# Two ternary feed-forward stages: input turned by DMA instead of TensorE, and the second product slipped between tiles of the first

## The chip, the cores and the metric

The kernel runs on one core of a Trainium2 chip. A core has five engines with a queue each: TensorE (PE in the profile; its weight loads are PEld), VectorE (DVE), ScalarE (ACT), GpSimd (POOL) and SyncE (SP, whose queue issues DMAs). The metric is the device time of one execution in microseconds (us). Before the change it is 2577.71 us, the median of 3 runs (2575.08 to 2578.1).

## What is computed

The input x has shape (8, 1024, 256), so 8192 tokens of 256 numbers. Six sublayers follow each other, each on a layer norm of x that is added back: a gated feed-forward layer with 4-bit weights, a decaying linear attention, the gated layer again, a ternary feed-forward layer, an attention with compressive memories, and the ternary layer again. The change touches the two ternary layers only:

```python
def _ternary(w):
    scale = jnp.maximum(jnp.mean(jnp.abs(w)), 1e-08)
    return jnp.clip(jnp.round(w / scale), -1.0, 1.0)   # in value
h = jnp.einsum('bsd,fd->bsf', x, _ternary(W1)) + b1    # 256 -> 1024
h = jax.nn.gelu(h, approximate=False)
out = jnp.einsum('bsf,df->bsd', h, _ternary(W2)) + b2  # 1024 -> 256
...
x = x + 0.5 * _L1_ffn_ref(_layernorm(x), W1, b1, W2, b2)
```

The ternary weights are exact in a reduced 32-bit format (fp32r) that TensorE multiplies faster than full fp32. The activations are not, so each is split into a rounded high part and a low part (the rest), and every product runs twice.

## The kernel before

x stays in SBUF for the whole kernel as 16 tiles X[g] of a group of 512 tokens each (128 partitions, G = 4 tiles of 128 tokens, 256 columns). `ffn_ternary(last, after)` (L1176) is called twice: L2093 after the second 4-bit layer, and L2095 as the last stage, where each finished group is also stored (L1273, in the last group tile by tile, L1271).

Its steps for a group g of 16:

- `norm(g)` (L1188): four VectorE instructions L1193 write the normalized tiles into xn, a tile with one buffer that all stages share.
- `norm_turn(g)` (L1205): eight TensorE transposes L1212 bring xn into two PSUM tiles pt. ScalarE rounds each to the high part xh (L1215), and VectorE subtracts it from pt to get the low part xl (L1217).
- `hidden(g)` (L1223): for each of eight slices f of 128 of the 1024 columns, four products L1231 (two halves k of the 256 inputs, xh and xl) into a PSUM tile ph; ScalarE applies Gelu with the bias into an SBUF tile hf (L1239) and rounds it to hh (L1240); VectorE subtracts to get hl (L1242).
- `down(g)` (L1252): for each of the four token tiles, sixteen products L1258 (eight slices, hh and hl) into a PSUM tile po, which VectorE adds to x with the factor 0.5 (L1266).
- `biased(j, g)` (L1200): VectorE adds half the output bias to a tile of x ahead of time (L1203).

The loop L1275 runs over g = 0 to 17; iteration g does norm_turn(g), hidden(g - 1) and down(g - 2). Work for VectorE is put between the slices of hidden as a list `between`: norm(g + 1), a share of the layer-norm statistics (`ln.advance(g)`), and near the end the first statistics of the next stage (`begin`). `PLANS` (L346) says in batches of how many groups the statistics are taken, and by which iteration. A tile's statistics are L235 and L236; a batch ends in twelve small instructions, L248 to L264.

PSUM holds two pt tiles, four ph tiles and two po tiles, eight banks in all.

What sets the order: a framework places the instructions of each engine by its own estimate of when they are ready, in the order written where several are. `order_keeper` (L200) makes a function `pin` that ties an instruction behind the last pinned one on its engine. A stage may enter the list `loose`; pinned instructions then stay behind those pinned before that stage, but are not tied to each other. The ternary stages are loose, and TensorE's instructions in them are not pinned at all, so the framework chooses their order. The engines then run the fixed order, and waits are semaphores.

The 4-bit layers already turn data by DMA (L940, L1116, `dma_start_transpose` on 16-bit data), and the SyncE queue issues those transposes and the stores.

Of the kernel before, what the change touches and what calls it, by code (L numbers as in the profile page):

```python
# [10 lines left out]
F32R = mybir.dt.float32r  # L11
BF16 = mybir.dt.bfloat16
I32 = mybir.dt.int32
AF = mybir.ActivationFunctionType
ALU = mybir.AluOpType
AX = mybir.AxisListType
# [7 lines left out]
G = 4  # L24
# [15 lines left out]
def macaron_kernel(  # L40
# [156 lines left out]
    )  # L197


    def order_keeper():  # L200

        last = {}

        def pin(ins):
            e = ins.ins.engine
            if e in last:
                tc.add_manual_dep(
                    ins.ins, last[e].name,
                    mybir.DependencyInfo(
                        mybir.DependencyClass.NoSync, mybir.DependencyReason.DATA  # L210
                    ),
                    reason="order",
                )
            if not loose:
                last[e] = ins.ins
            return ins

        def behind():

            st = ExitStack()  # L220
            for ins in last.values():
                st.enter_context(tc.issue_after(ins))
            return st

        return pin, behind
# [2 lines left out]

    loose = []
    scratch = []  # L230
    pin, behind = order_keeper()

    def tile_stats(xt, mv):
        st = ln_pool.tile([P, 6], F32, tag="ln_s1", name="ln_s1")
# [33 lines left out]
    def statistics(sizes, dues):  # L268
# [81 lines left out]
        "fp4": ((3, 1, 2, 4, 4, 2), [0 if g < 3 else G * (g - 2) + 2 for g in range(NG)]),  # L350

        "decay": ((2, 2, 4, 4, 4), [max(0, G * g - 5) for g in range(NG)]),
        "ternary": ((2, 2, 4, 4, 4), [max(0, g - 1) for g in range(NG)]),

        "memory": (
            (GB + 3, 3, 4, NG), [max(0, G * (g - GB) - 4) for g in range(NG)]
# [42 lines left out]
    def transpose_group(src, dst, psum, tag, both_act=False, pin=lambda ins: ins):  # L399

        for k in range(2):
            pt = psum.tile([P, TG], F32, tag=tag, name="pt")
            for j in range(G):
                pin(
                    nc.tensor.transpose(
                        pt[:, j * P : (j + 1) * P], src[:, j, k * P : (k + 1) * P], ident
                    )
                )
            if k == 0 or both_act:
                nc.scalar.copy(dst[:, k, :], pt)  # L410
            else:
                pin(nc.vector.tensor_copy(dst[:, k, :], pt))

    def fp4_first(xn, mg, pool):

# [760 lines left out]
    def ffn_ternary(last, after=None):  # L1176
        with ExitStack() as st:
            lnp = st.enter_context(tc.tile_pool(name="f1_ln", bufs=2))
            hp = st.enter_context(tc.tile_pool(name="f1_h", bufs=2))
            tp = st.enter_context(tc.tile_pool(name="f1_t", bufs=4))  # L1180
            ps_t = st.enter_context(tc.tile_pool(name="f1_pt", bufs=2, space=PSUM))
            ps_h = st.enter_context(tc.tile_pool(name="f1_ph", bufs=4, space=PSUM))
            ps_o = st.enter_context(tc.tile_pool(name="f1_po", bufs=2, space=PSUM))
            xns, xts, hs = {}, {}, {}
            ln, xns[0] = begun.pop("ternary")
            loose.append("ternary")

            def norm(g):  # L1188
                xn = xn_pool.tile([P, G, D], F32, tag="xn", name="xn")
                for j in range(G):  # L1190
                    n = G * g + j
                    pin(
                        nc.vector.tensor_scalar(  # L1193
                            xn[:, j, :], X[g][:, j, :], ln.mv[:, n, 0:1], ln.lr[:, n : n + 1],
                            ALU.subtract, ALU.mult,
                        )
                    )
                xns[g] = xn

            def biased(j, g):  # L1200

# [3 lines left out]
            def norm_turn(g):  # L1205
                xn = xns.pop(g)
                xh = lnp.tile([P, 2, TG], F32R, tag="xh", name="xh")
                xl = lnp.tile([P, 2, TG], F32R, tag="xl", name="xl")
                for k in range(2):
                    pt = ps_t.tile([P, TG], F32, tag="pt", name="pt")  # L1210
                    for j in range(G):
                        nc.tensor.transpose(  # L1212
                            pt[:, j * P : (j + 1) * P], xn[:, j, k * P : (k + 1) * P], ident
                        )
                    nc.scalar.copy(xh[:, k, :], pt)  # L1215
                    pin(
# [1 line left out]
                            xl[:, k, :], pt, xh[:, k, :].bitcast(F32), ALU.subtract  # L1218
                        )
                    )  # L1220
                xts[g] = (xh, xl)

            def hidden(g, between):  # L1223
                xh, xl = xts.pop(g)
                hh = hp.tile([P, NF, TG], F32R, tag="hh", name="hh")
                hl = hp.tile([P, NF, TG], F32R, tag="hl", name="hl")
                for f in range(NF):
                    ph = ps_h.tile([P, TG], F32, tag="ph", name="ph")
                    for k in range(2):
                        for xt in (xh, xl):  # L1230
                            nc.tensor.matmul(  # L1231
                                ph,
                                lhsT=w1[:, k, f * P : (f + 1) * P],
                                rhs=xt[:, k, :],
                                start=(k == 0 and xt is xh),
                                stop=(k == 1 and xt is xl),
                            )
                    hf = tp.tile([P, TG], F32, tag="hf", name="hf")
                    nc.scalar.activation(hf, ph, AF.Gelu, bias=b1c[:, f : f + 1])  # L1239
                    nc.scalar.copy(hh[:, f, :], hf)  # L1240
                    pin(
                        nc.vector.tensor_tensor(  # L1242
                            hl[:, f, :], hf, hh[:, f, :].bitcast(F32), ALU.subtract
                        )
                    )
                    if f < len(between):
                        between[f]()
                    elif f >= NF - G:
                        biased(f - NF + G, g)
                hs[g] = (hh, hl)  # L1250

            def down(g):  # L1252
                hh, hl = hs.pop(g)
                for j in range(G):
                    po = ps_o.tile([P, D], F32, tag="po", name="po")
                    for f in range(NF):
                        for ht in (hh, hl):
                            nc.tensor.matmul(  # L1258
                                po,
                                lhsT=ht[:, f, j * P : (j + 1) * P],  # L1260
                                rhs=w2[:, f, :],
                                start=(f == 0 and ht is hh),
                                stop=(f == NF - 1 and ht is hl),
                            )
                    pin(
                        nc.vector.scalar_tensor_tensor(  # L1266
# [2 lines left out]
                    )  # L1269
                    if last and g == NG - 1:  # L1270
                        nc.sync.dma_start(out=out_v[g][:, j, :], in_=X[g][:, j, :])  # L1271
                if last and g < NG - 1:
                    nc.sync.dma_start(out=out_v[g], in_=X[g])  # L1273

            for g in range(NG + 2):  # L1275
                between = []
                if g < NG:
                    norm_turn(g)
                    if g + 1 < NG:
                        between.append(lambda: norm(g + 1))  # L1280
                    between.append(lambda: ln.advance(g))
                    if after and g >= NG - 6:
                        between.append(lambda: begin(after, NG - g))
                if 0 <= g - 1 < NG:
                    hidden(g - 1, between)
                else:
                    for do in between:
                        do()
                if 0 <= g - 2 < NG:
                    down(g - 2)  # L1290
            loose.pop()


# [850 lines left out]
```

## Time and profile before

| | |
|---|---|
| median of 3 runs | 2577.71 us (2575.08 to 2578.1) |
| the profiled execution | 2575.58 us |
| its span, first to last instruction | 2573.8 us, mean granted TensorE clock 0.994 |
| first ternary stage, first to last product (L1231 to L1258) | 1473.06 to 1729.76 us |
| second ternary stage | 2312.70 to 2570.11 us |

The profile is of one execution. Busy time is counted per engine; idle time in front of a group of instructions is put down to what ended it. The chain of work that ended last is followed back from the last instruction, at each step to what released it. Matmul records overlap, because TensorE is pipelined: the distance between starts is what a product costs. VectorE instructions that follow each other without a wait overlap a little too.

### The profile page before, as it was taken

To read this page: it belongs to the slowest core of one execution; us is meant where nothing else is said; L and a number is where in the kernel's file an instruction comes from. 1 tells how busy PE (TensorE), PEld (TensorE's weight loads), DVE (VectorE), ACT (ScalarE), POOL (GpSimd) and SP (SyncE) were. 2 spreads that over 40 slices of the span, in tenths; PEclk is the share of its full clock that TensorE was granted. 3 is DMA by queue.
4 is the path that set the end of the run, shared out by engine and by line. 5 is a ranking of instruction groups with operands and counts; after the bars stand their busy time and mean duration, and the time that the engine had idled before them with its cause. 6 is when DMAs were issued, how large, how long until landed. Compare 5 with 4: busy or idle time off the path is not lost.

```text
span 2573.8 us, 53038 instructions
## 1 busy us (share of the span) xinstructions
PE 2477.9 (96%) x20426; PEld 1848.8 (72%) x20426; DVE 2082.0 (81%) x4809; ACT 1245.3 (48%) x2906; POOL 1019.4 (40%) x1282
## 2 busy tenths in 40 slices
PE   4899999989999999999999999999999999999999
PEld 2577777756666666677777689985666767778998
DVE  7798888758878778998888599648888888879864
ACT  5344444433333333444444376656555555437664
POOL 5677676621101004666667400005555555530000
PEclk9999999999999999999999999999999999999999
DMA  7456556500000002565566200000000000000101
GB/s 223 86 120 118 111 122 118 107 21 15 12 21 14 2 2 49 116 121 116 118 118 119 52 1 1 1 1 2 2 2 2 2 2 2 2 2 26 34 33 42
DMA packets 199901, 132.43 MB, mean 51 GB/s; under 512 B 138048, under 2 KB 174944, under 8 KB 199648
## 3 DMA queue, kind: packets, MB, share of 16 engines
q1 hardware_dynamic: 198704, 127.85, 23.2%
q8 instruction: 160, 2.62, 0.4%
q14 instruction: 93, 0.76, 0.1%
q0 software_dynamic: 240, 0.54, 0.1%
q10 hardware_dynamic: 704, 0.66, 0.1%
HBM read 80.77 MB, written 16.52 MB: 38 GB/s over the span
## 4 chain that ended last, share of the span: by engine, by line
PE 79%; DVE 12%; issue 3%; POOL 3%; ACT 3%; DMA 1%; SPq 0%; ACTq 0%; DVEq 0%; POOLq 0%
PE po L1258 9%; PE po L1001 9%; PE ph L1231 9%; PE pu L889 8%; PE pg L889 8%; PE sc L1301 5%; PE py L1385 5%; PE pq L1399 4%; PE pkv L1399 4%; PE pk L1399 4%; PE po L1399 4%; PE py L1367 2%; PE pmo L1824 2%; DVE at L1310 1%; DVE qp L823 1%
## 5 line engine op out<-in xcount | busy, mean ns | idle before, releaser
L889 PE MATMUL pu<-wgu,xt 128*128 128x352 f32 x1024 | 346.9, 461 | 9.2 <-DVE h L904 8.9
L889 PE MATMUL pg<-wgu,xt 128*128 128x352 f32 x1024 | 347.6, 462 | 7.3 <-ACT sg L899 7.0
L899 ACT ACTIVATE sg<-pg 128x352 f32<-128x352 f32 x256 | 118.1, 461 | 402.8 <-PE pg L889 377.6
L1001 PE MATMUL po<-wd,ht 128*128 128x256 f32 x1280 | 303.8, 385 | 0.7 <-DVE x L1006 0.6
L1001 PEld LDWEIGHTS po<-wd,ht 128*128 128x128 f32 x1280 | 246.7, 194 | 55.0 <-issue 3.0
L845 POOL TENSOR_TENSOR h<-h,q_rs 128x704 f32<-128x704 f32 (+1 forms) x128 | 176.2, 1377 | 264.0 <-DVE q_rs L830 263.8
L889 PEld LDWEIGHTS pu<-wgu,xt 128*128 128x128 f32 x1024 | 184.9, 191 | 111.1 <-issue 16.7
L889 PEld LDWEIGHTS pg<-wgu,xt 128*128 128x128 f32 x1024 | 185.6, 191 | 95.9 <-ACT sg L899 14.5
L1258 PE MATMUL po<-w,hl 128*128 128x256 f32 x1024 | 243.9, 280 | 1.2 <-DVE hl L1242 1.2
L1258 PE MATMUL po<-w,hh 128*128 128x256 f32 x1024 | 243.5, 280 | 0.1
L1940 POOL TENSOR_TENSOR mo<-mo 128x256 f32<-128x256 f32 x192 | 164.1, 855 | 195.7 <-DVE mo L1837 187.1
L1231 PE MATMUL ph<-xh,w 128*128 128x512 f32 x512 | 204.4, 401 | 1.5 <-ACT hf L1239 0.6
L955 POOL TENSOR_TENSOR ht<-gt,ht 128x768 f32<-128x768 bf16 x124 | 205.8, 1660 | 0.0
L1231 PE MATMUL ph<-xl,w 128*128 128x512 f32 x512 | 202.2, 396 | 0.0
L1242 DVE TENSOR_TENSOR hl<-hf,hh 128x512 fp32r<-128x512 f32 x256 | 168.7, 686 | 39.8 <-ACT hh L1240 36.2
L1258 PEld LDWEIGHTS po<-w,hl 128*128 128x128 f32 x1024 | 192.1, 188 | 4.4 <-DVE hl L1242 2.4
L1258 PEld LDWEIGHTS po<-w,hh 128*128 128x128 f32 x1024 | 192.0, 188 | 2.8 <-DVE x L1266 0.6
L1239 ACT ACTIVATE hf<-ph,b1c 128x512 f32<-128x512 f32 x256 | 168.3, 696 | 18.4 <-PE ph L1231 16.1
L1524 POOL TENSOR_TENSOR x<-x,ob 128x1024 f32<-128x1024 f32 x16 | 37.9, 2368 | 332.2 <-ACT xn L317 310.1
L1310 DVE TENSOR_TENSOR at<-sc,dec 128x512 f32<-128x512 f32 x256 | 158.6, 683 | 11.8 <-PE sc L1301 11.8
L1310 DVE TENSOR_TENSOR at<-sc,tri 128x512 f32<-128x512 f32 x256 | 165.0, 680 | 0.4 <-PE sc L1301 0.4
L914 DVE SCALAR_TENSOR_TENSOR h<-qp,h 128x704 f32<-128x704 f32 x124 | 110.3, 889 | 65.8 <-ACT qp L849 65.4
(291 smaller groups left out, 5691.7 us busy)
## 6 DMA issues: line engine op xcount, KB each, us to landing
ht<-sd SPq DMA_DIRECT2D x124, 384.0 KB
xt<-sd SPq DMA_DIRECT2D x56, 256.0 KB
sd<-sct SPq DMA_DIRECT2D x124, 64.0 KB
x<-in_x SPq DMA_DIRECT2D x15, 512.0 KB
out<-x SPq DMA_DIRECT2D x15, 512.0 KB
t_raw<-in_w_t SPq DMA_DIRECT2D x16, 256.0 KB
gt<-gd SPq DMA_TRANSPOSE x124
gtx<-xn SPq DMA_TRANSPOSE x56
```

Of the source, the lines that this page charges most:

```text
L845: pin(mul.tensor_tensor(vb, vb, rs[:, :, None].to_broadcast([P, nb, 16]), ALU.mult))
L889: nc.tensor.matmul(ps, lhsT=xts[g][:, 2 * j + k, :], rhs=wgu[:, k, (2 * q + of_up) * NHALF : (2 * q + of_up + 1) * NHALF], start=(k == 0), ...
L955: nc.gpsimd.tensor_tensor(wide.rearrange("p c t -> p (c t)"), grid.rearrange("p c t -> p (c t)"), wide.rearrange("p c t -> p (c t)"), ALU. ...
L1001: nc.tensor.matmul(po, lhsT=left, rhs=right, start=(n == 0), stop=(n == NC))
L1231: nc.tensor.matmul(ph, lhsT=w1[:, k, f * P : (f + 1) * P], rhs=xt[:, k, :], start=(k == 0 and xt is xh), stop=(k == 1 and xt is xl),)
L1239: nc.scalar.activation(hf, ph, AF.Gelu, bias=b1c[:, f : f + 1])
L1242: nc.vector.tensor_tensor(hl[:, f, :], hf, hh[:, f, :].bitcast(F32), ALU.subtract)
L1258: nc.tensor.matmul(po, lhsT=ht[:, f, j * P : (j + 1) * P], rhs=w2[:, f, :], start=(f == 0 and ht is hh), stop=(f == NF - 1 and ht is hl),)
L1301: nc.tensor.matmul(sc[:, m, :], lhsT=kt[rows, m, :], rhs=qz[rows, m], start=True, stop=True)
L1310: nc.vector.tensor_tensor(at, sc.rearrange("p m (e t) -> p (m e) t", e=2), weight, ALU.mult)
L1399: nc.tensor.matmul(dst, lhsT=lhsT, rhs=rhs, start=n == 0, stop=n == len(parts) - 1)
L1940: summed = nc.gpsimd.tensor_tensor(mo[:, :, :, 0, :], mo[:, :, :, 0, :], mo[:, :, :, m, :], ALU.add)
```

## The change

1. The input of groups 3 to 15 is no longer transposed by TensorE. `norm` writes xn into a tile of the stage's own. `planes_turned` has GpSimd copy the low and the high 16-bit words of the fp32 numbers into two planes (four copies of 512 words), and SyncE issues one DMA transpose of the 16 blocks of 128x128 words. An iteration later or more, `planes_joined` has GpSimd put the words together again as xf (four copies), ScalarE rounds xf to xh (one instruction of 1024 columns), and GpSimd, in place of VectorE, subtracts to get xl (four instructions of 256 columns). Groups 0 to 2 are still turned by TensorE, through ph tiles. For the others norm is done two groups ahead instead of one.
2. TensorE's instructions of the stage are tied in the order written, by an order keeper that is never loose (`own`).
3. `down(g)` now returns four pieces, one per token tile; `hidden` runs one of them after each second slice, so that 8 products L1231 and 16 products L1258 alternate. The tiles of down(g - 2) that stood behind hidden(g - 1) now stand inside it.
4. Gelu writes back into the PSUM tile ph; the rounding and VectorE's subtraction read it there. The tile hf is gone. PSUM now holds six ph tiles and two po tiles.
5. The plan of the statistics has smaller batches at the start (2, 2, 2, 2, 4, 4 groups), due an iteration earlier.

The core of the diff:

```diff
-        "ternary": ((2, 2, 4, 4, 4), [max(0, g - 1) for g in range(NG)]),
+        "ternary": (
+            (2, 2, 2, 2, 4, 4), [0 if g < 2 else 1 if g == 2 else g - 2 for g in range(NG)]
+        ),
...
+    def planes_turned(xn, pool):
+        words = xn.rearrange("p t d -> p (t d)").bitcast(U16).rearrange("p (n b) -> p n b", b=2)
+        apart = pool.tile([P, 2, G * D], U16, tag="apart", name="apart")
+        for b in range(2):
+            for half in (slice(0, G * D // 2), slice(G * D // 2, G * D)):
+                nc.gpsimd.tensor_copy(apart[:, b, half], words[:, half, b])
+        turned = pool.tile([P, 2, 2 * G, P], U16, tag="turned", name="turned")
+        nc.sync.dma_start_transpose(
+            out=turned.rearrange("p b n t -> p (b n) t"),
+            in_=apart.rearrange("p b n -> p (b n)"),
+        )
+        return turned
+
+    def planes_joined(turned, dst):
+        words = dst.rearrange("p k t -> p (k t)").bitcast(U16)
+        words = words.rearrange("p (k j t b) -> p b k j t", k=2, j=G, b=2)
+        for b in range(2):
+            for k in range(2):
+                nc.gpsimd.tensor_copy(
+                    words[:, b, k],
+                    turned[:, b].rearrange("p (j k) t -> p k j t", k=2)[:, k],
+                )
...
-            ps_t = st.enter_context(tc.tile_pool(name="f1_pt", bufs=2, space=PSUM))
-            ps_h = st.enter_context(tc.tile_pool(name="f1_ph", bufs=4, space=PSUM))
+            gp = st.enter_context(tc.tile_pool(name="f1_g", bufs=2))
+            ps_h = st.enter_context(tc.tile_pool(name="f1_ph", bufs=6, space=PSUM))
...
+            by_dma = lambda g: g > 2
+            own, _ = order_keeper(())
...
             def norm(g):
-                xn = xn_pool.tile([P, G, D], F32, tag="xn", name="xn")
+                if by_dma(g):
+                    xn = gp.tile([P, G, D], F32, tag="xn", name="xn", bufs=1)
+                else:
+                    xn = xn_pool.tile([P, G, D], F32, tag="xn", name="xn")
...
-                xns[g] = xn
+                xns[g] = planes_turned(xn, gp) if by_dma(g) else xn
...
+                if by_dma(g):
+                    xf = gp.tile([P, 2, TG], F32, tag="xf", name="xf", bufs=1)
+                    planes_joined(xn, xf)
+
+                    def split():
+                        nc.scalar.copy(xh, xf)
+                        for k in range(2):
+                            for half in (slice(0, TG // 2), slice(TG // 2, TG)):
+                                nc.gpsimd.tensor_tensor(
+                                    xl[:, k, half], xf[:, k, half],
+                                    xh[:, k, half].bitcast(F32), ALU.subtract,
+                                )
+
+                    return split
...
-                    hf = tp.tile([P, TG], F32, tag="hf", name="hf")
-                    nc.scalar.activation(hf, ph, AF.Gelu, bias=b1c[:, f : f + 1])
-                    nc.scalar.copy(hh[:, f, :], hf)
+                    nc.scalar.activation(ph, ph, AF.Gelu, bias=b1c[:, f : f + 1])
+                    nc.scalar.copy(hh[:, f, :], ph)
                     pin(
                         nc.vector.tensor_tensor(
-                            hl[:, f, :], hf, hh[:, f, :].bitcast(F32), ALU.subtract
+                            hl[:, f, :], ph, hh[:, f, :].bitcast(F32), ALU.subtract
                         )
                     )
                     if f < len(between):
                         between[f]()
                     elif f >= NF - G:
                         biased(f - NF + G, g)
+                    if tiles and f % 2:
+                        tiles.pop(0)()
...
             for g in range(NG + 2):
                 between = []
                 if g < NG:
-                    norm_turn(g)
-                    if g + 1 < NG:
-                        between.append(lambda: norm(g + 1))
+                    split = norm_turn(g)
+                    for m in (g + 1, g + 2):
+                        if m < NG and by_dma(m) == (m == g + 2):
+                            between.append(lambda m=m: norm(m))
                     between.append(lambda: ln.advance(g))
                     if after and g >= NG - 6:
                         between.append(lambda: begin(after, NG - g))
+                    if split:
+                        between.append(split)
+                tiles = down(g - 2) if 0 <= g - 2 < NG else []
                 if 0 <= g - 1 < NG:
-                    hidden(g - 1, between)
+                    hidden(g - 1, between, tiles)
...
```

All products L1231 and L1258 and the transposes of groups 0 to 2 are wrapped in `own(...)`.

## The prediction

> **What bounds the kernel now.** I read the busy times first, then the chain of work that ended last in order of time, then busy time by stretch, then groups of instructions inside one stretch.
>
> The page's busy line and two rows of its slices:
> ```profile
> PE 2477.9 (96%) x20426; PEld 1848.8 (72%) x20426; DVE 2082.0 (81%) x4809; ACT 1245.3 (48%) x2906; POOL 1019.4 (40%) x1282
> PE   4899999989999999999999999999999999999999
> POOL 5677676621101004666667400005555555530000
> ```
> TensorE is nearly always busy. GpSimd is idle where L1258 works: slices 23 to 26 and the last four are the two ternary stages. The chain there (start, length, what):
> ```profile
> 1595.97 0.88 PE pt L1212 x8
> 1596.85 7.47 PE ph L1231 x32
> 1604.32 7.54 PE po L1258 x64
> 1611.86 0.87 PE pt L1212 x8
> ```
> Only TensorE stands in it. A group is turned (0.87 us), multiplied by W1 (32 products, 7.47, 0.2334 each) and by W2 (64 products, 7.54, 0.1178 each): 15.88 us. Busy time by stretch (length; PE, PEld, DVE, ACT, POOL; granted clock): eight groups of the steady part, the first 17 us of the stage, a stretch of the memory stage, and 2 us just before the stage:
> ```profile
> 1556.66:1683.73 127.07, 127.07 (x835) 115.35 (x834) 98.52 (x255) 81.85 (x145) 0.00 (x0) 1.00 0.00 1
> ...
> 1473.00:1490.00 17.00, 15.37 (x78) 12.03 (x79) 17.00 (x69) 12.81 (x23) 0.00 (x0) 1.00 0.01 2
> ...
> 1850.00:2200.00 350.00, 346.00 (x4657) 244.91 (x4652) 294.73 (x669) 197.49 (x507) 196.00 (x268) 1.00 0.01 2
> ...
> 1460.00:1462.00 2.00, 2.00 (x6) 1.55 (x6) 0.00 (x0) 0.00 (x0) 0.00 (x0) 0.50 0.00 0
> ```
> In the steady part TensorE never rests; VectorE needs 12.3 and ScalarE 10.2 us of the 15.88. At the start it is the other way: VectorE is full and TensorE loses 1.6 us in 17. The last row is the clock at half, after a rest of 3.4 us.
>
> **The turns that go (removes).** Groups 3 to 15 lose their eight transposes in both stages: 2 x 13 x 0.87 = **-22.6 us**, if 15.01 us a group is then kept. This is nearly all that can be won.
>
> **What takes their place, per group.** VectorE loses two L1217 subtractions (0.68 each). GpSimd gets four copies of 128x512 16-bit words to split the planes, four to join them, four subtractions of 128x256. No row has such copies: from below 0.24 (L1086, 64 columns), from above 1.07 (L845, 512 columns, two operands). L1086 and L964 (0.289 at 128 columns) give 0.81 ns a column, so I take 0.60. For the subtraction 0.46 (L967, 128 columns) to 0.86 (L1940); I take 0.73 (L2027). Sum 8 x 0.60 + 4 x 0.73 = 7.7 us, bounds 3.8 and 12.0, below the 15.01 in every case: hidden.
>
> The Trainium skill, GPSIMD Engine Reference, Performance versus the Vector engine, gives a tight loop of 512 elements 769 ns; no run here shows that one, and eight copies by it would be 6.2 us, which is hidden too.
>
> SyncE issues one transpose of 16 blocks: 1.20 us for four blocks (L1116), 1.24 for six (L940), so some 1.43. Four blocks landed 4.77 us after their issue in the chain; sixteen take 4.8 to 19.1, I take 9. The chain of group g+2: norm done 3 us into iteration g, planes apart by 7.2 (at 1.07 each), landed by 26.3 at the worst, joined by 30.5, rounded and subtracted by 35; hidden(g+2) starts at 45. Ten microseconds stay over. In the last stage SyncE also holds out<-x, which waits for x of group g-2 at the end of iteration g; a transpose stuck behind it leaves 8 us later, and that still fits. So nothing is paid here.
>
> ScalarE: eight Gelus (0.69), eight roundings (0.63 from SBUF, 0.59 from PSUM by L1215) and one copy of 1024 columns (two L1215 are 1.18): 11.7 us of 15.01, hidden. Gelu into PSUM has no row; even 0.1 either way is 0.8 of 3.3 idle us.
>
> **The written order (moves).** Four switches between the halves per group replace one. Around 1699 us eight W1 products between W2 products took 1.92 instead of 1.87; at 1490.12, 1.86. So a switch pair costs 0 to 0.05: 15 groups x 3 x 2 stages = 0 to 4.5 us; I take **+0.5**, since most such rows show none.
>
> The order takes slack away. So far down(g-2) came 17.5 us after the last W1 product of its group (down 7.54, turn 0.87, hidden 7.47, 1.65 up to the eighth slice), against 2.0 for Gelu, rounding and subtraction. Now it comes after one tile (1.88), two products (1.87) and 1.65: 5.4 us. ScalarE and VectorE may lag 3.4 us instead of 15.5; enough in the steady part, not at the start.
>
> **The start of each stage.** TensorE's progress from 1472.9 to 1493.0, W1 products, then W2:
> ```profile
> 1472.90:1493.00 20.10, 14.59 (x56) 9.99 (x57) 1.00 0.01 2
> ...
> 1472.90:1493.00 20.10, 3.69 (x20) 3.18 (x20) 1.00 0.01 2
> ```
> Here W2 products are slipped in as slices of hl come. Written out, turn(1) precedes hidden(0), so TensorE waits for norm(1), done at 1475.3. hidden(0) follows to about 1483.6, but turn(2) needs norm(2) (1485.05 to 1486.4 in VectorE's timeline) and two PSUM buffers that subtractions free, and the first tile of down(0) needs all eight slices. VectorE has its first statistics, norm(2), now also norm(3) (four in 1.36 us) before the last slices: I put hl(0) complete at 1492.5 and the first tile done at 1493. By then 40 W1 and 16 W2 products are done against 56 and 20: 16 x 0.2334 + 4 x 0.1178 = 4.2 us, in the second stage too (the same 56 and 20 from 2312.5 to 2333). **+8.4**. It is no less than 0 if VectorE's order fills the gaps.
>
> Rests: some 2 us before turn(2) and 2 more behind it. The granted clock fell to 0.50 for 6.8 us after the rest of 3.4 us at 1454.8, and not in 1473 to 1490 with 1.6 us lost. Half clock for 6.8 us costs 3.4; I take 1.0 per stage of 0 to 3.4: **+2.0**.
>
> **VectorE's load.** Back to back, L1242 takes 0.62 (three in 1.86), L1193 0.34, L1203 0.38, L1266 0.42, a tile's statistics 0.38 + 0.16, a batch's terms 2.0. A group costs 5.0 + 1.4 + 1.5 + 1.7 = 9.6, plus statistics: the 10.6 of groups 8 to 11 fall into iterations 4 and 5, those of 12 to 15 into 6 to 9. So 14.9 in 4 and 5, 12.2 in 6 to 9, 9.6 behind (11.7 in the first stage, which prepares the next). And GpSimd now works beside it. Two-operand rows without GpSimd (1550 to 1700), then beside it (1850 to 2200, GpSimd busy 56%); the third reads SBUF once:
> ```profile
> L263 DVE TENSOR_TENSOR ln_h<-ln_h,ln_r 128x16 f32<-128x16 f32 x3 | 0.5, 160 | 0.0
> ```
> ```profile
> L263 DVE TENSOR_TENSOR ln_h<-ln_h,ln_r 128x16 f32<-128x16 f32 x6 | 1.7, 289 | 0.2
> L1994 DVE TENSOR_TENSOR rw<-rw,mw 128x80 f32<-128x80 f32 x40 | 14.4, 360 | 1.4
> L1310 DVE TENSOR_TENSOR at<-sc,tri 128x512 f32<-128x512 f32 x160 | 103.3, 681 | 0.0
> ```
> L263 grew by 0.13; L1994, at least 0.241, by 0.12 on average and 0.56 at most; L1310 is 0.683 in the decay stage, so unhurt. L1242 loses an SBUF operand and joins L1310's kind; four L1203 and, perhaps, four L1193 remain: 8 x 0.13 = 1.0 us. Iterations 4 and 5 then need 15.9 of 15.01 and the third tile's buffer comes late: I take 1.5 of 0 to 3 per stage, **+3.0**.
>
> A rule speaks against this part: the Trainium skill, SBUF — State Buffer, Who interferes with whom, says that VectorE with two SBUF inputs (or in a two-port mode, which tensor_scalar has) and GpSimd exclude each other for a whole instruction. By it each of the eight could wait a whole GpSimd piece, 0.73: 5.8 us instead of 1.0. The rows show that waits exist and are mostly shorter; I keep the rows.
>
> **Sum.** -22.6 + 0.5 + 8.4 + 2.0 + 3.0 = **-8.7**. The profiled execution took 2575.58 (span 2573.8 and 1.8 around it): **2566.9**, say 2567. The median, 2577.71, lies 2.1 higher. 0.2%, about what a measurement of this kernel can tell from no change, is 5.2 us.
>
> **Rivals.**
> A, the forecast: -4.9 to -16. Chance 0.52.
> B, the start eats it: 4.2 + 3.4 + 3.0 per stage and 4.5 of switches is 25.7, so +3, about 2578; -4.9 to +8. For it: VectorE without rest from 1473; against it: 3.4 us of lag are allowed. 0.20.
> C, slower: waiting for GpSimd makes VectorE the bound. It decides at 15.88 - 12.2 = 3.7 us of waits per group, 0.46 per instruction. At 0.6 (4.8 us) iterations 4 and 5 last 19.7, 6 to 9 17.0, the rest 16.5 and 15.01: +15.8 in the first stage, +6.9 in the second, +8.4 for the starts: +31, 2607; at 0.73, +51. For it: L1994's longest; against it: the means, 0.12 and 0.13. 0.18.
> D, the start costs nothing: down to -22.6, 2553. 0.10. That the change doesn't do what it says (planes later than TensorE) would need 10 us more than my worst chain and sits in C.
>
> **Numbers.** Faster by over 0.2%: 0.49 of A and all of D, 0.59; within: 0.03 of A and 0.15 of B, 0.18; slower: 0.05 of B and C, 0.23. The range runs from 2555 (most of D) to 2592 (A, B and the near part of C); some 0.16 is left out.
>
> **What would show it.** In the chain of the new profile a steady group of 7.47 + 7.54 us with no L1212 piece, and 15.0 us between groups; L1266 and the GpSimd copies absent from the chain; GpSimd some 8 us busy per group; at 1473 to 1495 some 40 W1 products where there were 56. L1203 above 0.9 us on average, or VectorE full in iterations 6 to 9, would make it C; half clock in both starts, B.

## The result, and the profile after

The change made the kernel slower. Its median is 2595.26 us (2594.23 to 2596.19, 4 runs) against 2577.25 us for the kernel before on the same chip; the ratio is 1.0072, 95% interval 1.0060 to 1.0084. The forecast was 2567 with a range of 2555 to 2592, so sign and range both failed. The profiled execution after took 2596.19 us, 20.6 us more than the one of before.

In the kernel after, the lines of the first ternary stage are L1225 (normalizing), L1235 (bias), L1280 (W1 products), L1291 (the subtraction that gives hl), L1311 (W2 products), L1320 (addition to x), L423 and L437 (GpSimd's splitting and joining copies) and L1250 (GpSimd's subtraction); L236 are statistics. The page's busy line, the slices of TensorE and GpSimd, and the engines' shares of the chain that ended last:

```profile
PE 2477.1 (95%) x20218; PEld 1839.8 (71%) x20218; DVE 2085.1 (80%) x4781; ACT 1253.9 (48%) x2880; POOL 1240.2 (48%) x1594
...
PE   4899999989999999999999898999999999999899
...
POOL 4677676621110004666666455414555555535541
...
PE 69%; DVE 20%; POOL 3%; issue 3%; ACT 2%; DMA 2%; SPq 0%; ACTq 0%; POOLq 0%; DVEq 0%
```

TensorE has 208 instructions fewer (the turns), but there is an 8 in slices 23, 25 and 38 (counted from one): at the start of the first ternary stage and inside both stages. Before, these slices had a 9. VectorE's share of the chain is 20%, up from 12%. The steady part is what was forecast; the chain there (start, length, what) holds nothing but products, 3.75 us for two slices and a down tile:

```profile
1648.16 1.88 PE po L1311 x16
1650.04 1.87 PE ph L1280 x8
1651.91 1.88 PE po L1311 x16
1653.80 1.87 PE ph L1280 x8
```

Sixty microseconds earlier it looks like this:

```profile
1585.27 0.41 DVE x L1320
1585.68 1.59 DVE xn L1225 x4
...
1588.66 0.60 DVE hl L1291
1589.26 0.33 DVE x L1320
1589.59 2.29 DVE x L1235 x3
1591.88 1.55 DVE xn L1225 x2
1593.43 0.59 DVE hl L1291
1594.02 1.59 DVE xn L1225 x2
1595.61 0.33 DVE ln_s L236
1595.94 0.32 DVE x L1320
1596.26 0.61 DVE hl L1291
...
1596.91 0.58 PE po L1311
1597.50 3.26 PE ph L1280 x8
```

VectorE is never idle here, and TensorE waits twice for a subtraction (2.6 us from 1591.5, 2.0 us from 1594.9). Ahead of it stand bias additions and normalizing for groups that TensorE reaches tens of microseconds later. The 3.26 us for eight products that take 1.87 in the steady part is TensorE at half clock: the granted clock was 0.50 from 1593.6 to 1600.4. By stretch (length; PE, PEld, DVE, ACT, POOL; granted clock, DMA share, GB/s), the two starts of the stages and what follows:

```profile
1473.00:1505.00 32.00, 26.98 (x133) 21.96 (x132) 31.11 (x111) 20.57 (x35) 7.76 (x12) 0.89 0.14 28
1505.00:1600.00 95.00, 87.03 (x535) 76.90 (x534) 93.68 (x262) 58.77 (x96) 57.49 (x81) 0.97 0.22 42
1600.00:1700.00 100.00, 97.71 (x601) 87.16 (x600) 62.48 (x142) 67.52 (x114) 42.56 (x60) 0.96 0.12 22
2327.00:2360.00 33.00, 28.50 (x140) 23.06 (x139) 31.76 (x113) 21.76 (x37) 7.62 (x12) 0.90 0.17 33
2360.00:2560.00 200.00, 192.04 (x1205) 171.31 (x1205) 147.58 (x357) 131.83 (x215) 101.39 (x144) 0.98 0.27 64
```

The same of the kernel before, with the second stage's first 32 us as the third row:

```profile
1473.00:1505.00 32.00, 30.37 (x156) 24.40 (x157) 32.00 (x116) 25.79 (x45) 0.00 (x0) 1.00 0.00 1
1505.00:1600.00 95.00, 95.00 (x638) 86.77 (x637) 91.96 (x291) 60.70 (x108) 0.00 (x0) 1.00 0.00 1
2313.00:2345.00 32.00, 30.26 (x154) 24.05 (x153) 31.80 (x115) 25.18 (x43) 0.00 (x0) 1.00 0.00 1
```

Length less PE is idle TensorE; length times (1 - clock) is what the clock took, roughly, since the clock is given in hundredths. So the starts cost 5.0 - 1.6 + 3.5 = 6.9 and 4.5 - 1.7 + 3.3 = 6.1; behind them 8.0 + 2.3 + 8.0 = 18.2 us are idle and some 2.9 + 4.0 + 4.0 = 10.9 went with the clock. With the turns' -22.6 that makes +19.5, against +20.6 measured. TensorE's waits behind the start, two rows for the first stage and one for the second (us in total, times, longest):

```profile
PE po L1311 <- DVE hl L1291: 9.6, 7, 2.6
PE po L1311 <- ACT hh L1289: 0.4, 1, 0.4
PE po L1311 <- DVE hl L1291: 7.8, 5, 2.3
```

So 17.4 of the 18.2 us are waits for that subtraction, and the question is why VectorE is late with it.

### The profile page after: what moved, and what is told of

The parts are those of the page before. It is cut to its first block, busy times and chain, and to the rows that moved or that the text cites. A ratio compares the mean times of both kernels' runs of the same rounds, so it can differ in the third digit from the quotient of the medians.

```text
span 2594.4 us, 53047 instructions
## 1 busy us (share of the span) xinstructions
PE 2477.1 (95%) x20218; PEld 1839.8 (71%) x20218; DVE 2085.1 (80%) x4781; ACT 1253.9 (48%) x2880; POOL 1240.2 (48%) x1594
## 4 chain that ended last, share of the span: by engine, by line
PE 69%; DVE 20%; POOL 3%; issue 3%; ACT 2%; DMA 2%; SPq 0%; ACTq 0%; POOLq 0%; DVEq 0%
PE po L1029 9%; PE pu L917 8%; PE pg L917 8%; PE po L1311 5%; PE ph L1280 5%; PE sc L1358 5%; PE py L1442 5%; PE po L1456 4%; PE pq L1456 4%; PE pkv L1456 4%; PE pk L1456 4%; DVE hl L1291 2%; PE py L1424 2%; DVE xn L1225 2%; DVE ln_s L236 2%
## 5 line engine op out<-in xcount | busy, mean ns | idle before, releaser
L1311 PE MATMUL po<-w,hl 128*128 128x256 f32 x1024 | 250.5, 282 | 17.6 <-DVE hl L1291 17.4
L1291 DVE TENSOR_TENSOR hl<-ph,hh 128x512 fp32r<-128x512 f32 x256 | 174.6, 683 | 107.3 <-ACT hh L1289 106.1
L1311 PE MATMUL po<-w,hh 128*128 128x256 f32 x1024 | 248.2, 281 | 0.6 <-ACT hh L1289 0.4
L1288 ACT ACTIVATE ph<-ph,b1c 128x512 f32<-128x512 f32 x256 | 170.3, 668 | 154.3 <-PE ph L1280 150.3
L1311 PEld LDWEIGHTS po<-w,hl 128*128 128x128 f32 x1024 | 193.4, 189 | 26.3 <-DVE hl L1291 20.8
L1280 PE MATMUL ph<-xh,w 128*128 128x512 f32 x512 | 208.2, 407 | 0.0
L1280 PE MATMUL ph<-xl,w 128*128 128x512 f32 x512 | 207.8, 406 | 0.0
L1311 PEld LDWEIGHTS po<-w,hh 128*128 128x128 f32 x1024 | 193.5, 189 | 7.5 <-issue 0.7
```

Source lines behind the costliest of these rows:

```text
L1280: nc.tensor.matmul(ph, lhsT=w1[:, k, f * P : (f + 1) * P], rhs=xt[:, k, :], start=(k == 0 and xt is xh), stop=(k == 1 and xt is xl),)
L1288: nc.scalar.activation(ph, ph, AF.Gelu, bias=b1c[:, f : f + 1])
L1291: nc.vector.tensor_tensor(hl[:, f, :], ph, hh[:, f, :].bitcast(F32), ALU.subtract)
L1311: nc.tensor.matmul(po, lhsT=ht[:, f, j * P : (j + 1) * P], rhs=w2[:, f, :], start=(f == 0 and ht is hh), stop=(f == NF - 1 and ht is hl),)
```

## The experiments

Ratios are to the kernel before, run on the same chip beside each; differences between experiments are made from these. Three theories to begin with. **O**: the framework's fixed order puts normalizing and bias of later groups ahead of the subtractions that TensorE waits for. **L**: GpSimd lengthens VectorE's instructions, and that alone fills VectorE. **S**: the written order costs at the starts.

### e1_tied: VectorE's work tied in written order, statistics free

```diff
+            tie, _ = order_keeper(())
+            line = lambda ins: tie(pin(ins))
...
-                pin(nc.vector.tensor_tensor(xj, xj, b2h, ALU.add))
+                line(nc.vector.tensor_tensor(xj, xj, b2h, ALU.add))
```

The same for normalizing, both subtractions and the addition to x.

> VectorE's main line (normalizing, high and low parts, bias, additions to x) is tied in the order written; the statistics stay free. Theory O (the framework places normalizing and bias of later groups ahead of subtractions that TensorE waits for): they can no longer run ahead, the excess in the first ten groups goes, 2565 to 2578 us. Theory L (GpSimd's pieces make VectorE's instructions longer, and that alone fills VectorE): the waits stay, 2590 to 2600. Theory S (TensorE's written order at the start of each stage is what costs): 2588 to 2600.

2570.84 us, ratio 0.9973 (0.9962 to 0.9984): the order alone turns the loss into a gain, some 25 us from after. Over both stages normalizing took 641 ns on average here, more than after's 507 (the bias 470 against 522), so it was not the lengthening that went. The time is in the range that O gave.

### e2_no_gpsimd: GpSimd's work left out

```diff
-            in_=apart.rearrange("p b n -> p (b n)"),
+            in_=words.rearrange("p n b -> p (n b)"),
...
-                    planes_joined(xn, xf)
+                    xf = X[g].rearrange("p t d -> p (t d)").rearrange("p (k t) -> p k t", k=2)
...
+                        nc.scalar.copy(xl, xf)
```

It leaves out the splitting, the joining and GpSimd's subtraction, so that the stages multiply something else.

> Leaves out the splitting and joining of the planes and the subtraction on GpSimd; the products of groups 3 to 15 take both parts as copies of x by ScalarE, and the DMA transpose runs but nothing reads it. VectorE and TensorE have the same instructions as in the changed kernel. L: VectorE's normalizing back to 0.41 us and the bias to 0.42, TensorE without rests after the first 30 us of a stage: 2562 to 2574 us. O: normalizing and bias still run ahead, still above 2585. S: as O.

2566.0 us, ratio 0.9959 (0.9944 to 0.9973): in the range that L gave, and far below the 2585 that O gave. So neither theory is right as it was stated. VectorE's groups from 1473 to 1593 (busy us, mean ns, idle before), normalizing and bias, of the kernel before, of after and of e2:

```profile
L1193 DVE TENSOR_SCALAR xn<-x,ln_mv,ln_r 128x256 f32<-128x256 f32 x36 | 13.1, 408 | 0.1
L1203 DVE TENSOR_TENSOR x<-x,b2h 128x256 f32<-128x256 f32 x40 | 15.8, 415 | 0.0
```
```profile
L1225 DVE TENSOR_SCALAR xn<-x,ln_mv,ln_r 128x256 f32<-128x256 f32 x50 | 22.8, 511 | 0.0
L1235 DVE TENSOR_TENSOR x<-x,b2h 128x256 f32<-128x256 f32 x40 | 21.6, 553 | 0.0
```
```profile
L1221 DVE TENSOR_SCALAR xn<-x,ln_mv,ln_r 128x256 f32<-128x256 f32 x53 | 18.8, 413 | 2.0 <-DMA turned<-xn 2.0
L1231 DVE TENSOR_TENSOR x<-x,b2h 128x256 f32<-128x256 f32 x36 | 14.0, 415 | 0.0
```

In e2 normalizing runs ahead as far as in after (53 instructions, over 13 groups, while TensorE is in the eighth), and TensorE is busy 95.00 of 95 us from 1505 to 1600. So running ahead without GpSimd does no harm behind the start, and e18 below shows that GpSimd's waits, somewhat shorter there, do none either without running ahead. It takes both: VectorE was nearly full there before, too (91.96 of 95 us), with no room for 50 x 0.10 + 40 x 0.14 = 10.6 us of waits. e2 removes more than the waits (nothing in it depends on GpSimd), so it does not part the two by itself.

### e3_order_only and e4_dma_only: the change's two halves

```diff
-            by_dma = lambda g: g > 2
+            by_dma = lambda g: False
```

> All groups turned by TensorE; the written order, the tiles of the second product between the first, Gelu in PSUM and the plan of statistics stay. S: the start of a stage alone costs what is lost, 7.5 us by the twentieth microsecond and more behind it: 2590 to 2605 us. L: only the start's 4 to 8 us per stage: 2583 to 2593, and no rest of TensorE after 1510. O: like L, since one buffer for the normalized tiles keeps normalizing from running ahead.

2584.17, ratio 1.0032 (1.0022 to 1.0043). TensorE is full from 1505 on and loses at the starts (30.03 of 32 at clock 0.95; 26.54 of 31 at 0.94): the written order costs there, less than S said.

```diff
-            own, _ = order_keeper(())
+            own = lambda ins: ins
...
-                    if tiles and f % 2:
-                        tiles.pop(0)()
```

> Groups 3 to 15 turned by DMA, but TensorE in the framework's order and the second product behind the first as before, so some 15 us of lag are allowed. If the small slack of the written order is what turns VectorE's lag into rests of TensorE: 2553 to 2565 us. L in its strict form (VectorE has more than TensorE's time to do in the first ten groups, whatever the order): 2575 to 2595.

2591.22, ratio 1.0056 (1.0041 to 1.0071). With TensorE's order free TensorE is still idle for 6.1 of 95 us, VectorE busy 94.14. The time is in the range that L gave. The small slack of the written order is not the cause by itself: TensorE rests without it, too.

### e5_tied_free and e6_bias_loose: which part of the tie

e5 is e1 with e4's edit; e6 is e1 with the bias left to the framework:

```diff
-                line(nc.vector.tensor_tensor(xj, xj, b2h, ALU.add))
+                pin(nc.vector.tensor_tensor(xj, xj, b2h, ALU.add))
```

> TensorE's order is the framework's again (no down tile inside the hidden part), and VectorE's is tied as in e1_tied. O (VectorE works ahead of its turn): with VectorE tied, the only loss left is the start of the stages, which the undone turn alone put at 2584.2 - 2576.8 = 7.4 us; without the written order on TensorE most of it returns, so 2563 to 2568. S' (the written order is what makes the tie work, because two products lie between a first half and its second): 2575 to 2592, as in e4_dma_only.

> Tied as e1_tied, but the bias additions may again go where the framework puts them; normalizing, subtractions and down additions stay in written order. If it is the bias additions that run ahead and fill VectorE (four a group, 0.52 us each, free to go as soon as X is there): 2585 to 2596. If it is the normalizing (four a group and, behind each group's, GpSimd's copies and the transfer, which bring the next GpSimd work forward): 2568 to 2574, the time of e1_tied.

e5: 2577.27, ratio 0.9998 (0.9989 to 1.0007). The guess that the start's cost would return was wrong: once VectorE is tied, TensorE's written order is worth some 6 us. e6: 2574.98, ratio 0.9990 (0.9981 to 0.9999): of the 25 us between after and e1, normalizing's (and the subtractions') place is some 21 and the bias's some 4, which is not clear of noise (the intervals of e6 and e1 overlap).

### e7_whole_pieces: the small pieces undone

```diff
-            for half in (slice(0, G * D // 2), slice(G * D // 2, G * D)):
-                nc.gpsimd.tensor_copy(apart[:, b, half], words[:, half, b])
+            nc.gpsimd.tensor_copy(apart[:, b], words[:, :, b])
```

Likewise two joining copies for four, and one subtraction of 1024 columns for four.

> GpSimd's four splitting copies of a group become two, its four joining copies two, its four subtractions one; nothing else. L (a VectorE instruction waits for the GpSimd instruction before it to end): a wait is as long as half the piece, so normalizing rises from a mean of 507 ns to 600 or more, bias from 522 to 620, and with VectorE full in the first ten groups of both stages the time rises by 40 groups' share, to 2600 to 2612. If waits go by the total of GpSimd's time (words share the port): means unchanged and 2592 to 2598.

2607.71, ratio 1.0116 (1.0099 to 1.0133). GpSimd's work became shorter, 2 x 1.08 + 2 x 1.42 + 2.45 = 7.4 us a group against 9.0, and the kernel slower. From 1473 to 1750, normalizing and bias:

```profile
L1232 DVE TENSOR_TENSOR x<-x,b2h 128x256 f32<-128x256 f32 x64 | 39.7, 634 | 0.0
...
L1222 DVE TENSOR_SCALAR xn<-x,ln_mv,ln_r 128x256 f32<-128x256 f32 x60 | 26.9, 504 | 1.6 <-POOL apart L422 1.6
```

and their durations (minimum, median, maximum; first and last start), those of after's bias from 1473 to 1593 below:

```profile
L1232 DVE TENSOR_TENSOR x<-x,b2h x64: 380/416/2607, 1475.8 to 1641.2; 128x256 f32<-128x256 f32 x64
```
```profile
L1235 DVE TENSOR_TENSOR x<-x,b2h x40: 380/414/968, 1474.5 to 1590.9; 128x256 f32<-128x256 f32 x40
```

The median is untouched in both; a few instructions wait, and the longest wait grew from 0.55 to 2.2 us, nearly the length of the new subtraction (2.446). So an instruction that meets a GpSimd piece waits for all that is left of it, and the piece's length sets the worst stall. The traces show it one by one: of normalizing and bias in the first stage, the 23 in e7 and the 38 in after that took over 0.52 us all end 0.14 to 0.29 us behind the end of a GpSimd piece. The expectation had the mean right for the bias (620) and wrong for normalizing (600, it stayed at 504). This is the rule of the Trainium skill, SBUF — State Buffer, Who interferes with whom: whoever is first has the shared ports for the whole instruction. The subtraction from PSUM, with one SBUF input, took 682 to 686 ns on average in every kernel with GpSimd's pieces and 689 and 690 in e2 and e3 without them, so it is not lengthened, as that section also says.

### e8_bias_gpsimd: less work for VectorE, more for GpSimd

```diff
-                pin(nc.vector.tensor_tensor(xj, xj, b2h, ALU.add))
+                nc.gpsimd.tensor_tensor(xj, xj, b2h, ALU.add)
```

> The bias additions go from VectorE to GpSimd (four of 256 columns, some 0.75 us each by the subtraction of the same size: 3.0 us a group, GpSimd 12 of 15). L: VectorE loses 4 x 0.52 = 2.1 us a group, is no longer full in the first ten groups, and the loss there goes: 2576 to 2584, the start's cost alone. O: normalizing still runs ahead and waits become more frequent: 2585 to 2596. A third way: GpSimd becomes late with the next group's planes, above 2600.

2611.14, ratio 1.0131 (1.0117 to 1.0145), the third way. VectorE from 1473 to 1750:

```profile
L1225 DVE TENSOR_SCALAR xn<-x,ln_mv,ln_r 128x256 f32<-128x256 f32 x60 | 35.8, 653 | 16.7 <-POOL apart L423 16.7
```

VectorE has less to do, yet stands still for 16.7 us: normalizing, again ahead of its turn, waits for xn's one buffer, which GpSimd's copies free late (bias additions are queued ahead of them), and the subtractions are queued behind it. GpSimd's bias additions in turn waited 30.5 us for normalizing.

### e9 to e12: two edits that did not help

e9 has an even plan of the statistics, e10 is e1 with the transposes of groups 1 and 2 written later, e11 and e12 are e1 with the plan and with both.

```diff
-            (2, 2, 2, 2, 4, 4), [0 if g < 2 else 1 if g == 2 else g - 2 for g in range(NG)]
+            (2, 2, 2, 2, 2, 2, 2, 2), [0 if g < 2 else 1 if g == 2 else g - 2 for g in range(NG)]
...
-                    split = norm_turn(g)
+                    later = g in (1, 2)
+                    split = None if later else norm_turn(g)
...
+                    if later:
+                        between.insert(0, between.pop())
+                        between.insert(1, lambda: norm_turn(g))
```

> Only the plan of the statistics is changed, (2, 2, 2, 2, 4, 4) to eight pairs of groups, each due two groups ahead: groups 10, 11, 14 and 15 are counted two to four groups later, at the price of two more sets of terms (some eight small VectorE instructions each). VectorE's order stays the framework's. O (what runs ahead and in whatever order fills VectorE in the first ten groups): work that cannot run ahead any more leaves room, so part of the loss returns: 2580 to 2590. If the framework fills the room with more normalizing and bias, no change: 2592 to 2597.

> Tied as e1_tied; besides, the transposes of groups 1 and 2 are written behind the first two first-half products of the group before, not ahead of them. S (the written order holds back the first products of a stage for the next group's transposes): TensorE's first products start earlier and 2 to 6 us of the two starts return, 2564 to 2569. If VectorE sets the start (it was busy 31.8 of the first 32 us in e1_tied), nothing returns: 2569 to 2573.

> Tied as e1_tied, with the even plan of the statistics. VectorE's load in the first twelve groups falls by some 4 x 0.57 = 2.3 us a pair of groups put off: the stalls left between 1505 and 1600 (3.3 us of idle TensorE in e1_tied's three windows, and as much in the other stage) go, 2563 to 2568. If those stalls come from the waits on GpSimd alone and not from the load, 2569 to 2573.

> Both edits of e10_tied_turn_later and e11_tied_even_stats on the tied kernel. If the two causes are apart their gains add: 2558 to 2566. If both only move the same VectorE work, as much as the better of the two.

2600.7 (ratio 1.0095, 1.0078 to 1.0112), 2573.9 (0.9988, 0.9979 to 0.9997), 2578.44 (1.0008, 0.9998 to 1.0017), 2580.08 (1.0018, 1.0008 to 1.0029): none gained. e9, e11 and e12 lie outside all their ranges, e10 just above the one for no gain. The plan did not do what it says: all 76 statistics were done by 1640 in e11 as in e1, because they are free and the framework puts them early whatever their due time. What e11 lost may be the added sets of terms. Moving the transposes gained nothing at the start: the wait in front of them (1.9 us in e1) went, but one of 2.5 us for a subtraction, in front of W1 products, came instead, and TensorE was busy 27.57 of the first 32 us as in e1.

### e13 to e15: the statistics tied as well

e13 keeps the stage out of `loose`, so that all of VectorE's work is in written order; e14 is e1 with batches (2, 2, 4, 4, 4); e15 is e13 with e9's plan.

```diff
-            loose.append("ternary")
...
-            loose.pop()
```

> All of VectorE's work of the stages in written order, the statistics and their terms too; the plan is the change's. O for the statistics (they run ahead as normalizing did, and the rest of the stalls is theirs): the idle TensorE of e1_tied between 1505 and 1600 (3.1 us, and 3.6 in the other stage) goes: 2562 to 2569. If a burst of four statistics and a set of terms in one place of the written order holds up the subtractions more than their running ahead did: 2575 to 2590.

> Tied as e1_tied, statistics free, groups 4 to 7 as one set: five sets of terms in place of six. If what e11_tied_even_stats lost (7.6 us for two sets more) was the sets' small instructions, which wait for GpSimd one after the other, a set less gives 2 to 4 us: 2566 to 2569. If e11 lost by the order alone: 2569 to 2574.

> e13_all_tied with the even plan, which only now decides when the statistics are done. If load in the first ten groups is what counts, putting them off helps: 1 to 4 us below e13. If the two sets more count: 3 to 8 us above e13.

e13 took 2605.02 (1.0112, 1.0095 to 1.0129), e14 2575.86 (0.9992, 0.9981 to 1.0003), e15 2603.02 (1.0106, 1.0091 to 1.0121), which is not clear of e13. e13 and e14 lie above all their ranges. Written order as such is no cure. e13's chain behind the start, and below it TensorE's wait at the start (us in total, times, longest):

```profile
1537.28 2.74 DVE xn L1224 x4
1540.02 0.59 DVE hl L1290
1540.61 0.35 DVE ln_s L236
...
1545.91 0.32 DVE x L1319
...
1546.27 3.60 PE po L1310 x16
```
```profile
PE pt L1259 <- DVE hl L1290: 9.2, 2, 8.2
```

Ten tiles' statistics, 5.3 us, stand in one place ahead of the addition that frees TensorE's buffer. Most of e13's loss is a longer pile of the same kind at the starts: from 1490.65 to 1498.88 eight tiles' statistics and a set of terms stand ahead of one subtraction, TensorE waits 8.2 us, and of the first 32 us it is busy 19.08 at clock 0.79. Theory O has to be changed: what counts is not whether work is ahead of its turn but **how much VectorE work stands ahead of a result that TensorE needs next**, against the 3.75 us of two slices and a tile. Running ahead is one way to get such a pile, a burst in the written order is another. e14 did not gain from one set of terms fewer, so e11's loss stays unexplained.

### e16 to e18: the same work dealt out

e16 is e13 with a tile's normalizing behind each of the first four subtractions and the iteration's statistics and terms dealt over all eight; e17 deals the normalizing alone, statistics free.

```diff
-                            between.append(lambda m=m: norm(m))
+                            for j, do in enumerate(norm(m)):
+                                between[j].append(do)
...
+                    shares = ln.plan.get(g, ())
+                    for i, do in enumerate(shares):
+                        between[i * NF // len(shares)].append(do)
```

> As e13_all_tied (all of VectorE in written order), but the four normalizing instructions of a group stand behind the first four subtractions, one behind each, and the iteration's statistics and terms are dealt over the eight. Bursts (a stall is what stands between two subtractions beyond the 3.75 us of two pairs of products): with some 2.2 us ahead of each subtraction none is over, the stalls of e13 go, and the time is 2562 to 2572. If the written order of the statistics itself costs (no gap is filled by what comes later): 2580 to 2605.

> As e1_tied (statistics free), but the four normalizing instructions stand one behind each of the first four subtractions. Bursts: e1's remaining stalls (3.1 us between 1505 and 1600, 3.6 in the other stage, most behind four normalizing instructions in a row, 1.6 to 2.5 us) go: 2563 to 2568. If they come from the free statistics: 2569 to 2573.

e16: 2578.08, ratio 0.9997 (0.9988 to 1.0007), between its two ranges; e17: 2574.2, ratio 0.9985 (0.9976 to 0.9995), just above its second. By stretch, e16:

```profile
1473.00:1505.00 32.00, 25.86 (x112) 20.57 (x113) 30.21 (x99) 18.77 (x32) 6.55 (x10) 0.79 0.09 17
1505.00:1600.00 95.00, 95.00 (x611) 85.75 (x610) 84.54 (x226) 66.39 (x109) 50.94 (x74) 1.00 0.22 40
1600.00:1700.00 100.00, 100.00 (x639) 90.03 (x638) 79.42 (x192) 70.66 (x118) 50.33 (x76) 1.00 0.14 27
```

Behind the start TensorE never stops, in the second stage neither (215.00 of 215 from 2345): the piles were the cause. But the start got worse, 25.86 of 32 at clock 0.79, where e17, which differs in the statistics alone, has 27.02 at 0.89: statistics now stand between the first products. e17 kept stalls (TensorE 14.92 of 16 and 42.23 of 44 us in 1540 to 1600): as e16, with the statistics dealt out too, has none, those that e1 had left come from the free statistics. So e18 has e1's first three iterations and e16's order from the fourth on (the edit is against e17):

```diff
+                    if g == 3:
+                        loose.pop()
...
-                                between[j].append(do)
+                                between[at if g < 3 else j].append(do)
```

> The first three iterations as in e1_tied (statistics free, normalizing as a group), from the fourth on as in e16_spread_all (everything in written order, dealt behind the subtractions). If bursts and start are two causes: TensorE full from 1505 on as in e16, e1's start, so e1's time less the some 6 us of stalls it had left: 2563 to 2568. If the free statistics of the first iterations run ahead and only move the stalls: 2569 to 2578.

2564.17 us (2558.03 to 2569.75, 6 runs), ratio 0.9957 (0.9942 to 0.9972): faster than both kernels and as expected. Its profiled execution was its fastest, 2558.03:

```profile
1473.00:1505.00 32.00, 29.34 (x162) 24.16 (x161) 31.58 (x104) 25.02 (x42) 11.29 (x17) 0.97 0.20 34
1505.00:1600.00 95.00, 95.00 (x607) 85.55 (x606) 83.77 (x224) 65.26 (x107) 53.30 (x79) 1.00 0.19 34
1600.00:1700.00 100.00, 100.00 (x643) 90.23 (x642) 76.75 (x184) 72.98 (x122) 43.21 (x66) 1.00 0.15 27
```

VectorE's instructions done from 1473 to 1593 (8 slices and 4 of each other kind make a group; the statistics are 76 in the whole stage, 20 of them for the next):

| | hl | normalizing | bias | statistics |
|---|---|---|---|---|
| before | 64 | 36 | 40 | 76 |
| after | 54 | 50 | 40 | 60 |
| e1_tied | 59 | 40 | 28 | 74 |
| e18_start_free | 64 | 36 | 32 | 49 |

After had normalized 12.5 groups when it had subtracted 6.8; e18 keeps all of them in step. Its normalizing and bias still take 490 and 465 ns in this stretch, so the waits for GpSimd are still there and no longer matter.

## Why the prediction was wrong

The step that failed is **VectorE's load**, "Iterations 4 and 5 then need 15.9 of 15.01 and the third tile's buffer comes late: I take 1.5 of 0 to 3 per stage, +3.0", and with it "ScalarE and VectorE may lag 3.4 us instead of 15.5; enough in the steady part". Both sums take each iteration's VectorE work as done in that iteration. The stage was loose, so the framework had VectorE do later groups' work first, and a subtraction waited behind it. In place of +3.0 the runs show 18.2 us of idle TensorE and some 10.9 of half clock behind the stalls. e16 and e18, with the same instructions dealt out, have neither behind the start.

- **Turns gone, -22.6**: right. In e18 only the starts stand against it, by its first row 2.7 - 1.6 + 1.0 = 2.1, and 3.3 - 1.7 + 1.6 = 3.2 in the second stage (28.73 of 32 at 0.95): -17.3, and its profiled run, the fastest of six, is 17.5 below before's. Its median is only some 11 below that of before beside it; what its slower runs lose was not traced.
- **What takes their place**: GpSimd 9.0 us a group instead of 7.7 (0.67 and 0.80 a copy, 0.78 a subtraction); the transposes landed 4.3 us after issue (the median of 26; the longest 5.5) where 9 was taken; ScalarE's copy 1.05 instead of 1.18. All hidden, as said.
- **Switches, +0.5**: none seen; the alternation runs at 1.87 and 1.88.
- **The start, +8.4 and +2.0**: 34 W1 and no W2 products by 1493, not 40 and 16. The two starts cost 6.9 + 6.1 = 13.0 us with the clock, against 10.4. That this is near is partly luck: TensorE did wait in front of the transposes (1.9 us at 1475.0 and 2.6 at 1488.8), but e10, with them later, gained nothing. What stands among VectorE's first instructions decides more (e16 against e17).
- **Waits, 1.0 us a group**: the size was right, 4 x 0.10 + 4 x 0.14 = 0.96. What was missed is that so small a mean matters where VectorE is full already: before, it was busy 91.96 of 95 us from 1505 to 1600.
- **Rival C** named the right engine with the wrong condition: 0.46 us of wait per instruction was said to decide, and with the framework's order 0.12 was enough. Of its two signs VectorE was full (44.00 of 44 us from 1556), but the bias took 0.59 us there, not 0.9.

Left open: why e11 lost 8 us to e1 and e14 gained nothing, and what sets the rest of the starts' cost. Normalizing kept back by its buffers instead of by order was not tried.

## What to carry to other kernels

When an engine that feeds TensorE is near full for some stretch, its load per iteration says little: look at what its fixed order puts ahead of the next result that TensorE needs, and deal the other work between those results in amounts smaller than the slack. Count per stretch how far each kind of work has come; a kind that is many groups ahead shows the pile before any wait does. A change that makes the instructions of an almost full engine longer, even by 0.1 us each, should come with an order for that engine.

## What the runs showed of the hardware

- A VectorE normalizing or bias instruction (128x256, in SBUF) that meets a GpSimd piece waits for the piece to end: up to 0.55 us with pieces of 0.6 to 0.8 us and up to 2.2 us with a piece of 2.45. The median instruction waits not at all (0.41 us in after as in before).
- A GpSimd piece carries some 0.2 us that does not grow with its size, estimated from the medians of after and e7, which waits lengthen less than the means: 512 columns of 16-bit words were split in 0.617 and 1024 in 1.042 (2 x 0.617 - 1.042 = 0.19), joined in 0.772 and 1.372 (0.17); a subtraction of 256 columns took 0.742 and of 1024 2.396 ((4 x 0.742 - 2.396) / 3 = 0.19).
- Rests of TensorE of 2.3 and 2.6 us in after (at 2444.6 and 1591.5) were followed by half clock for 6.8 us (eight W1 products in 3.26 instead of 1.87 us), so that behind the starts the clock cost 0.6 us for each us of stall. The length of a rest does not settle it: after's rests of 1.1 and 1.7 us were not followed by half clock, but neither were rests of 3.1 and 3.2 us in e11 (at 1543.2 and 1594.3), and after's half clock from 1631.2 followed three rests of 0.5 to 0.9 us within 3 us.
